# One more attention stack beside layer 1's dispatch, and one attention step of layer 0 ahead of its first expert block

## The chip, the cores and the metric

The kernel runs on one core of one Trainium2 chip. The metric is the device time of one execution in microseconds. The core has five engines that each work through their own queue of instructions in order: TensorE (PE, with its weight loads as PEld), VectorE (DVE), ScalarE (ACT), GpSimd (POOL) and SyncE (SP, which here only issues transfers). Engines wait for one another by semaphores. Transfers (DMA) are issued by SP, ACT or POOL and then run on their own.

## The reference, cut to what matters

The input x has 32 sequences of 256 tokens with 128 features, so 8192 tokens. Two layers follow one another, each of the form x + s·silu(g), where s is an attention and g a mixture of experts, both on the normalised x:

```
xn = layernorm(x)
s  = L0 attention(xn)          # 16 heads of 8; product of two causal score matrices, no softmax
g  = silu(L0 experts(xn))      # 8 experts, the top 2 per token, plus a shared expert
x  = x + s * g
xn = layernorm(x)
s  = L1 attention(xn)          # 16 heads of 8; every 4th key and the keys within 8, softmax
g  = silu(L1 experts(xn))      # 8 experts, the top 2, at most 2048 tokens each
x  = x + s * g
```

In both layers the attention needs nothing of that layer's routing, and the experts need nothing of its attention. Only the last line of a layer joins them.

## The kernel before, in words

Tokens are handled in 16 packs of 512 (two sequences each). All of a layer's expert work goes through memory: each token's normalised row is scattered to the slots of its two experts (`disp0` in layer 0, `disp` in layer 1), the expert blocks read these slots, and their results are scattered back (`moe0`, `moe`) and read again by the step that combines them.

**Layer 0.** `attention0` (line 850) is a generator cut into 256 steps, eight for each sequence. `step()` (line 1032) runs one of them and counts it in `at`. The program strews these steps over the other work: two for each pack after the first while packs are loaded and normalised (30 steps), 12 beside the routing, then 103 beside the dispatch (line 1079, 128 indirect scatters issued by POOL, a step behind four of every five), then 71 beside the experts (line 1085, a step at every fourth yield of `experts()`), and the last 40 with `combine0` of the packs. The step run at yield 0 of the experts is number 145 counted from 0. Within sequence 18 it is the second of eight steps: it finishes sequence 17 (the 16 value matmuls of line 813, the copy `yT` of line 838, the output projection of line 842, the copy of line 844 and, as 17 is the second sequence of its pack, the 512 KB write of `part`, issued by ACT, line 847) and it starts the projections of sequence 19 (matmuls of line 727 and the two DVE products of line 732).

`experts()` (line 914) works off 71 blocks of 256 rows. Block i first transposes its rows (`xdt`, line 926), copies them (`xdT`, line 928) and yields. Then come the up matmuls (`eup`, line 935) with their activations (`ha`, line 940), and the down matmuls of the block before (`edn`, line 948). `fetch` (line 902) brings a block's weights by an indirect transfer from POOL and its rows by SP. The rows wait for all 128 scatters (`out0.behind(get)`, line 911). The transposes of block 0 are set behind the last ordered matmul that PE got so far (line 924).

**How the order is set.** Most instructions pass through `inline` (line 256), which ties each to the one before it on its engine, so that these stay in the order in which the program gives them. The rest is placed by a planner. In layer 1 the order of PE is exactly that of the program (`manual_schedule`).

**Layer 1.** `Attention` (line 287) works in 64 *stacks* of 128 query rows, two for each sequence, each advanced by `next(att.steps)` and counted in `begun`. Stack n computes the scores of its own rows (`apsc`, lines 378 and 384), their softmax weights (DVE lines 395 and 396, ACT line 398), and finishes stack n−1: transposes `apsT` (line 406), copies `apT` (line 408), value products `apav` (line 415). Along the way it prepares the next sequence (`prepare`, line 317). In the first stack of a sequence this includes the four DVE products `akb` (line 347), behind the stack's softmax work. Eight stacks run beside the end of layer 0, four beside `route1`, and 34 beside the dispatch (loop of line 1162, three or four scatters issued for each), so that `begun` is 46. The scatters go out three at a time, and POOL waits for the three before (`pace`, line 146).

Then come the 32 expert blocks of layer 1 (line 1169), with no attention beside them. Each block reads its rows by SP once all scatters have landed (line 1176), and its PSUM tiles (pool `pm`) take the banks that the scores had (pool `ps_s`, closed at line 1166). Last come the 18 stacks that are left, beside `combine` (line 1225) of the 16 packs. `combine` has three parts: reading the result rows, then sum and tanh, then products and output. The sums and products are on POOL (on DVE for the last pack), the tanh on ACT. Its buffers are three deep. `plan` (line 1250) says behind which of the remaining stacks each part stands: pack p of the first 12 at int(p·gap)+0, +2 and +3 with gap = (64 − begun)/13, the others at (4p − begun)+2, +6 and +7 (for pack 12 this is 4, 8 and 9). ACT and DVE take the parts in that order, between the stacks' own instructions.

Of the kernel before, what the change touches and what calls it, by code (L numbers as in the profile page):

```python
# [51 lines left out]
def some(g, n):  # L52
    for _ in range(n):
        next(g, None)
# [3 lines left out]
def model_kernel(ctx: ExitStack, tc: tile.TileContext, a: dict, out: bass.AP):  # L58
# [483 lines left out]
    with ExitStack() as c0:  # L542
# [155 lines left out]
        def dispatch():  # L698
            for k in range(2):
                if k:  # L700
                    nc.gpsimd.tensor_scalar(xr[:, :, P], xr[:, :, P], float(-T), None, ALU.add)
                    nc.gpsimd.tensor_copy(xr[:, :, P + 1], gate0[:, 1, :])
                for n in range(NT):
                    out0.put(slot0[:, k, n : n + 1], xr[:, n, :], NB * TB)
                    yield
# [111 lines left out]
        def shared(p, so):  # L817

            hs = ka.tile([P, NFC, PT], F32, tag="hs", name="hs", bufs=1)
            for f in range(NFC):  # L820
                psu = mm_tile("psu")
                inline(nc.tensor.matmul(psu, lhsT=upw[:, f * P : (f + 1) * P], rhs=xTs[p],
                                 start=True, stop=True))
                inline(nc.scalar.activation(hs[:, f, :], psu, AF.Gelu, bias=upb[:, f : f + 1]))
                yield
            dn = mm_tile("dn").rearrange("p (i c) -> p i c", i=TT)
            for i in range(TT):
                for f in range(NFC):
                    inline(nc.tensor.matmul(dn[:, i, :], lhsT=hs[:, f, i * P : (i + 1) * P],
                                     rhs=dnw[:, f, :], start=(f == 0), stop=(f == NFC - 1)))  # L830
            inline(nc.vector.scalar_tensor_tensor(so[:, 1], dn, 0.1, bc(dnb, 1, TT), ALU.mult, ALU.add))
            yield
# [199 lines left out]
        def step():  # L1032
            nonlocal at, sh
            p, n = at // 16, at % 16
            if n == 0:
                sos[p] = kso.tile([P, 2, TT, P], F32, tag="so", name="so")
                sh = shared(p, sos[p])
            next(gen)
            if n % 2 == 0:
                some(sh, 1)  # L1040
            if n == 15:
                for _ in sh:
                    pass
            at += 1
# [4 lines left out]
        BLOCK = 4  # L1049
# [29 lines left out]
        for n, _ in enumerate(dispatch()):  # L1079
            if n % 5 != 4:  # L1080
                step()
            if n % 8 == 0:
                some(wipe, 1)
        ek = ce.enter_context(tc.tile_pool(name="ek0", bufs=2))
        for n, _ in enumerate(experts()):
            if n % BLOCK == 0:
                step()
        ce.close()
        bk = c0.enter_context(tc.tile_pool(name="bk0", bufs=4))
# [7 lines left out]
        begun = 0  # L1097
# [19 lines left out]
        att = Attention(ctx, {p: sres[:, p * TT : (p + 1) * TT, :] for p in range(EARLY)})  # L1117
# [19 lines left out]
    def dispatch1(m):  # L1137
        for k, n in todo[:m]:
            if (k, n) == (0, 0):
                nc.gpsimd.tensor_scalar(xr[:, :, P], xr[:, :, P], float(T), None, ALU.add)  # L1140
                nc.gpsimd.tensor_copy(xr[:, :, P + 1], gate[:, 0, :])
            out1.put(sidx[:, k, n : n + 1], xr[:, n, :], E * CAP)
        del todo[:m]
# [17 lines left out]
    with tc.manual_schedule(engines={mybir.EngineType.PE}):  # L1161
        while todo:
            dispatch1(4 if len(todo) > NT // 4 else 3)
            next(att.steps)
            begun += 1
    cs1.close()


# [191 lines left out]
```

## Time and profile before

| what | us |
|---|---|
| median of 4 runs | 1935.88 (1916.36, 1935.78, 1935.98, 1937.61) |
| the profiled execution, its own time | 1940.79 |
| its span, first to last instruction | 1939.0 |
| PE busy | 1805.0 (93% of the span) |
| DVE busy | 1177.1 (61%) |
| ACT busy | 961.9 (50%) |
| POOL busy | 849.2 (44%) |
| layer 0's experts begin on PE | 459.88 |
| layer 1's experts begin on PE | 1525.16 |
| the last 18 stacks begin on PE | 1769.82 |

A line of the timeline has the start and the length of an instruction in us, its engine, its line in the kernel, the operation, what it writes and reads, its shape, a count where like ones were merged, and in brackets how long the engine sat idle before and who released it. A line of the table by stretches has the stretch, its length, then busy time and number of instructions of PE, PEld, DVE, ACT and POOL, the clock that PE was granted (1.00 is full speed), the busy share of the DMA engines, and GB/s. The last scatter is followed by the issue of the first row reads on SP (SPq).

### The profile page before, as it was taken

What the parts mean: (1) busy time and instruction counts of PE and PEld (TensorE: products, weight loads), DVE (VectorE), ACT (ScalarE), POOL (GpSimd) and SP (SyncE); (2) the same over time, 40 slices, a digit from 0 to 9 for tenths busy, and PEclk for the clock granted to TensorE, in tenths of its full rate; (3) what the DMA queues carried; (4) which work ended last, traced back from release to release, by engine and by line L of the source; (5) the groups of instructions that cost most, each with busy time, mean ns of one, the idle gap of its engine ahead of it and who ended that gap; (6) DMA issues with size and microseconds to landing.
All of it is one profiled execution on the core that took longest, in us unless ns stands there. A gap on an engine that the chain in (4) does not pass through costs nothing.

```text
span 1939.0 us, 45909 instructions
## 1 busy us (share of the span) xinstructions
PE 1805.0 (93%) x18616; PEld 1394.5 (72%) x18616; DVE 1177.1 (61%) x2227; ACT 961.9 (50%) x2180; POOL 849.2 (44%) x991
## 2 busy tenths in 40 slices
PE   5999999997999999999887799999999799999997
PEld 4777777775888878888765576677777576777665
DVE  6659667664333334433577587888888433335886
ACT  5433333333444444545354475567767333335776
POOL 3001554553444454544545530044554355554554
PEclk8999999998999999999988877899999899999988
DMA  8911111112343443434334410121011122222333
GB/s 282 382 49 37 62 56 41 43 44 63 119 149 123 127 142 119 150 123 137 117 104 142 139 48 7 62 74 35 31 34 33 54 70 68 72 67 84 100 113 90
DMA packets 127524, 183.86 MB, mean 95 GB/s; under 512 B 16340, under 2 KB 83183, under 8 KB 127312
## 3 DMA queue, kind: packets, MB, share of 16 engines
q1 hardware_dynamic: 96096, 92.45, 16.2%
q0 software_dynamic: 28336, 79.73, 12.3%
q10 hardware_dynamic: 2880, 8.74, 1.2%
q8 instruction: 147, 2.41, 0.5%
q14 instruction: 65, 0.53, 0.1%
HBM read 104.11 MB, written 78.00 MB: 94 GB/s over the span
## 4 chain that ended last, share of the span: by engine, by line
PE 31%; ACT 7%; DVE 6%; DMA 2%; issue 2%; POOL 2%; SPq 0%; ACTq 0%; DVEq 0%; POOLq 0%
PE mpsu L1186 6%; PE mpsd L1200 6%; PE apsc L378 3%; PE apsT L406 3%; ACT apT L408 3%; PE apav L415 3%; ACT apr L398 2%; PE apsc L384 1%; PE apsk L338 1%; DMA rows<-moe 1%; PE apsq L350 1%; PE apsv L358 1%; DVE apr L396 1%; PE mpst L1179 1%; DVE amx L395 1%
## 5 line engine op out<-in xcount | busy, mean ns | idle before, releaser
L166 POOL DMA_INDIRECT moe<-od,to x270 | 269.8, 999 | 124.8 <-issue 71.1
L777 ACT COPY qk<-ptr 128x512 f32<-128x512 f32 x256 | 138.1, 588 | 242.0 <-PE ptr L775 241.7
L792 DVE TENSOR_TENSOR pat<-pp,dmask 128x1024 f32<-128x1024 f32 x128 | 156.4, 1222 | 109.9 <-PE pp L790 109.9
L408 ACT COPY apT<-apsT 124x512 f32<-124x512 f32 x256 | 143.1, 584 | 102.9 <-PE apsT L406 102.0
L395 DVE TENSOR_REDUCE amx<-apsc 128x4 f32<-128x496 f32 x256 | 170.6, 666 | 38.0 <-PE apsc L384 37.9
L790 PE MATMUL pp<-qk 64*128 64x128 f32 x2048 | 172.6, 297 | 17.0 <-DVE pat L792 15.3
L790 PEld LDWEIGHTS pp<-qk 64*128 64x128 f32 x2048 | 136.9, 194 | 59.6 <-issue 43.1
L396 DVE TENSOR_TENSOR apr<-apsc,amx 128x496 f32<-128x496 f32 x256 | 172.6, 674 | 9.0
L940 ACT ACTIVATE ha<-eup,wt 128x256 f32<-128x256 f32 x284 | 119.0, 471 | 111.9 <-PE eup L935 58.2
L166 POOL DMA_INDIRECT disp<-xr,slot x128 | 134.1, 1048 | 62.8 <-POOL breath L150 26.1
L744 DVE TENSOR_TENSOR feat<-rot 128x1024 f32<-128x1024 f32 x128 | 158.6, 1280 | 3.9
L935 PE MATMUL eup<-xdT,wt 128*128 128x256 f32 x568 | 150.3, 390 | 10.9 <-ACT od L954 6.8
L406 PE MATMUL apsT<-ident,apr 128*124 128x128 f32 x1024 | 150.5, 293 | 9.6 <-ACT apr L398 4.9
L775 PE MATMUL ptr<-ident,feat 128*128 128x128 f32 x1024 | 146.9, 287 | 8.0 <-DVE feat L744 8.0
L166 POOL DMA_INDIRECT disp<-xr,sidx x128 | 126.7, 990 | 55.1 <-POOL breath L150 25.5
L415 PE MATMUL apav<-ava,apT 124*64 124x9 f32 x4096 | 142.6, 205 | 0.0
L415 PEld LDWEIGHTS apav<-ava,apT 124*64 124x64 f32 x4096 | 136.0, 139 | 8.8 <-issue 8.6
L948 PEld LDWEIGHTS edn<-wt,ha 128*128 128x128 f32 x1136 | 137.8, 192 | 3.6
L948 PE MATMUL edn<-wt,ha 128*128 128x128 f32 x1136 | 138.1, 275 | 0.0
L775 PEld LDWEIGHTS ptr<-ident,feat 128*128 128x128 f32 x1024 | 114.8, 145 | 30.2 <-issue 13.7
L406 PEld LDWEIGHTS apsT<-ident,apr 128*124 128x124 f32 x1024 | 121.3, 148 | 17.5 <-ACT apr L398 10.2
L935 PEld LDWEIGHTS eup<-xdT,wt 128*128 128x128 f32 x568 | 99.7, 190 | 45.0 <-issue 27.7
(250 smaller groups left out, 3344.7 us busy)
## 6 DMA issues: line engine op xcount, KB each, us to landing
disp<-zero SPq DMA_DIRECT2D x17, 1040.0 KB, 8.3
rows<-moe SPq DMA_DIRECT2D x64, 256.0 KB, 5.2
xd<-disp SPq DMA_DIRECT2D x71, 130.0 KB, 2.3
xd<-disp SPq DMA_DIRECT2D x32, 260.0 KB, 2.8
x<-in_x SPq DMA_DIRECT2D x32, 256.0 KB, 4.5
moe<-zero SPq DMA_DIRECT2D x8, 1024.0 KB, 14.9
part<-so ACTq DMA_DIRECT2D x16, 512.0 KB, 3.4
soin<-part SPq DMA_DIRECT2D x16, 512.0 KB, 4.4
```

Of the source, the lines that this page charges most:

```text
L166: ins = order(lambda: nc.gpsimd.indirect_dma_start(out=self.dst[:, :], out_offset=bass.IndirectOffsetOnAxis(ap=idx, axis=0), in_=rows, in_ ...
L395: inline(nc.vector.tensor_reduce(mx, sv, AX.X, ALU.max))
L396: inline(nc.vector.tensor_tensor(to, sv, bc(mx, 2, NK), ALU.subtract))
L406: nc.tensor.transpose(psT[:NK, j, :], pr[:, 4 * g + j, :], ident)
L408: inline(nc.scalar.copy(pT[:NK], psT[:NK]))
L415: nc.tensor.matmul(avv[u * QB : (u + 1) * QB, h, :], lhsT=pT[:NK, j, u * QB : (u + 1) * QB], rhs=va[:NK, 2 * st + u, h, :], start=True, st ...
L744: inline(eng.tensor_tensor(f[:, n].rearrange("p (h i j) -> p h i j", i=D, j=D), bc(r[:, n], 3, D), bc(r[:, 2 + n], 2, D), ALU.mult))
L775: inline(nc.tensor.transpose(pst[:, 2 * n + c], seq.feat[c][:, n, m * P : (m + 1) * P], ident))
L790: inline(nc.tensor.matmul(pp[:, w, i, c], lhsT=qk[r, 2 + c], rhs=qk[r, c], start=True, stop=True))
L792: inline(nc.vector.tensor_tensor(pat.rearrange("p w i c q -> p (w i c) q"), pp.rearrange("p w i c q -> p (w i c) q"), bc(dmask, 1, 8), ALU ...
L935: nc.tensor.matmul(pu, lhsT=wt[:, f * P : (f + 1) * P], rhs=xdT, start=True, stop=True)
L948: nc.tensor.matmul(psd[:, s, :], lhsT=hl[:, f, s * P : (s + 1) * P], rhs=wl[:, FF + f * P : FF + (f + 1) * P], start=(f == 0), stop=(f == ...
```

## The change

One step of layer 0's attention, number 145, is put in front of the experts (and in front of the pool that they open) and taken away at their yield 0. All later steps stay where they were. In layer 1 one stack, number 46 counted from 0, is put behind the dispatch loop, in front of the expert blocks. It is the first stack of a sequence. The remaining 17 stacks then run at the end, with `begun` at 47, from which `plan` is worked out anew.

```
                 step()
             if n % 8 == 0:
                 some(wipe, 1)
+        step()
         ek = ce.enter_context(tc.tile_pool(name="ek0", bufs=2))
         for n, _ in enumerate(experts()):
-            if n % BLOCK == 0:
+            if n and n % BLOCK == 0:
                 step()
...
             dispatch1(4 if len(todo) > NT // 4 else 3)
             next(att.steps)
             begun += 1
+
+        next(att.steps)
+        begun += 1
     cs1.close()
```

More of the change, by code (lines that the diff above doesn't have):

```diff
@@ L1083, in model_kernel @@
                 some(wipe, 1)
+        step()
         ek = ce.enter_context(tc.tile_pool(name="ek0", bufs=2))
         for n, _ in enumerate(experts()):
-            if n % BLOCK == 0:
+            if n and n % BLOCK == 0:
                 step()
@@ L1165, in model_kernel @@
             begun += 1
+        next(att.steps)
+        begun += 1
     cs1.close()
```

## The prediction

> **What bounds the kernel now.** I read the page first: PE is busy 1805.0 of 1939.0 us, so time is won where PE idles or where work comes off its path. The table of busy time by stretches shows where it idles.
>
> ```profile
> 450.00:460.00 10.00, 0.12 (x1) 0.16 (x2) 0.00 (x0) 0.52 (x1) 3.54 (x6) 0.70 0.22 59
> 460.00:945.00 485.00, 474.13 (x4017) 396.16 (x4018) 184.42 (x299) 233.64 (x585) 226.84 (x280) 1.00 0.40 126
> ...
> 1514.00:1525.00 11.00, 0.04 (x1) 0.00 (x0) 1.36 (x4) 1.08 (x3) 3.93 (x5) 0.57 0.21 66
> 1525.00:1770.00 245.00, 244.84 (x1410) 175.49 (x1411) 88.82 (x127) 80.16 (x188) 125.92 (x154) 0.99 0.23 66
> 1770.00:1939.00 169.00, 147.91 (x2086) 109.18 (x2084) 130.47 (x248) 119.97 (x245) 83.78 (x67) 0.92 0.36 104
> ```
>
> There are two holes of 10 and 11 us, each just ahead of a stage of experts. These stages are PE-bound (474 of 485 us, 245 of 245), so a later or earlier start is carried through them. The last stretch is not full: PE 148 of 169 us. The timeline shows what ends the first hole.
>
> ```profile
> 452.99 0.10 POOL L150 MEMSET breath<- 128x1 f32 x1 [1.36 <-DMA disp<-xr,slot]
> ...
> 454.99 0.97 POOL L166 DMA_INDIRECT disp<-xr,slot  x1 [0.30 <-issue]
> 457.62 37.65 SPq L910 DMA_DIRECT2D xd<-disp  x8
> ...
> 459.88 0.66 PE L926 MATMUL xdt<-ident,xd 128*128 128x128 f32 x2 [10.08 <-DMA xd<-disp]
> ...
> 460.46 1.08 PE L813 MATMUL y<-pat,vz 128*32 128x128 f32 x16
> ...
> 464.20 1.94 PE L935 MATMUL eup<-xdT,wt 128*128 128x256 f32 x8
> ```
>
> PE waits for the last scatter and the rows behind it. Then step 145 (from 460.46) stands between the transposes and the first up matmuls. The second hole:
>
> ```profile
> 1512.05 1.98 PE L415 MATMUL apav<-ava,apT 124*64 124x9 f32 x60
> ...
> 1519.76 0.98 POOL L166 DMA_INDIRECT disp<-xr,sidx  x1 [0.63 <-POOL breath L150]
> 1522.41 26.86 SPq L1175 DMA_DIRECT2D xd<-disp  x6
> ...
> 1525.16 1.94 PE L1179 MATMUL mpst<-ident,xd 128*128 128x128 f32 x8 [11.12 <-issue]
> ```
>
> The stacks end at 1514.03 and the rows come at 1525.16. The scatters are paced by their own landings (three per 5.7 us or more), not by the stacks.
>
> **The step.** It removes nothing; step 145 moves from behind the first transposes into the hole. On PE it is 16 value, 2 projection and 4 output matmuls. A like step at full clock (431.84 on) shows 0.64, 1.13 and 0.61 us, about 2.4; at 460.46, after the hole, they take 1.08, 2.08 and 1.06. Without it the up matmuls could start when xdT is copied (460.57 + 0.42, and 0.2 for the signal: 461.2) instead of about 464.0: 2.8 us. PE was slow there, until about 465.7, and the hole that is left (some 7 us) is long enough for the same to follow. The slow time then falls on other work, and only the step's full-clock price counts: 2.8 × 2.38/4.22 = 1.6 us. So the gain lies between 1.6 and 2.8; I take 2.0.
>
> On DVE its two products (1.29 us) come off 463.59 into idle time (DVE had idled 11.4 us); on ACT two copies of 0.37 us likewise. No POOL or SP instruction moves: expert weights were asked for from 188.2 on, and the row reads on SP wait for the scatters alone. But the step issues one transfer, the 512 KB write of part on ACT's queue, so far at 464.85, now at about 452.6, beside the last two scatters (issued 453.72 and 454.99). Six such writes stand within the dispatch (204.36, 245.68, 286.99, 328.30, 369.70, 411.00). POOL's next wait for its scatters was 1.50, 2.98, 3.58, 3.27, 1.69 and 1.66 us, where about 1.5 is the rule: 0 to 2.1 more, 0.95 on average. The row reads come later by that much; I take 1.0. Net −1.0 us, bounds −2.8 and +0.5 (−1.6 + 2.1).
>
> **The stack.** Stack 46 leaves the end, where it runs from 1769.82 to 1777.63 (7.8 us), and enters the second hole. Its like is the stack at 1498.12, also the first of a sequence: PE runs 8.2 us, the last softmax product on DVE ends 8.6 after the start, akb 10.1, the last DVE product (ao) 10.6. From 1514.1 this gives PE free at 1522.3, the score banks (which the expert tiles take over) free at 1522.7, DVE free at 1524.7. The rows arrive at 1525.16 and DVE is first wanted at 1526.28. The cover is the wait for the last scatter; the margins are 2.8, 2.4 and 1.6 us. Without the cover, were the rows there at 1514, the move would cost what it saves. It adds no transfer and no POOL work, and its akb starts (1522.6) after the last scatter was issued. So the experts start as before, and 7.8 us go at the end.
>
> Does PE start faster, with 2.8 us of hole instead of 11? After the 11 us the first 8 transposes took 1.94 us (later 4 take 0.60) and the first three up matmuls 2.38 (later 1.29): 0.74 + 1.09 = 1.8 us to win, 2.0 with the signal waits. The nearest row is the 1.78 us pause of PE at 1843.7: 16 score matmuls after it still took 1.48 instead of 1.09 us. I take 0, bounds −2.0 and 0.
>
> [...]
>
> **The combines.** What is late next is the end. gap falls from 18/13 to 17/13, and 16 combines lie over 17 stacks. Worked out from plan, the tanh parts of packs 0 to 11 stood behind stacks 2, 3, 4, 6, 7, 8, 10, 11, 13, 14, 15, 17 and those of 12 to 14 behind 8, 12, 16: one pair, at 8. Now they stand behind 2, 3, 4, 5, 7, 8, 9, 11, 12, 13, 15, 16 and 7, 11, 15: three pairs. The pair at 8 is visible:
>
> ```profile
> 1842.41 1.09 PE L406 MATMUL apsT<-ident,apr 128*124 128x128 f32 x8
> 1843.34 0.39 PE L426 MATMUL apsf<-wqkvo,aoT 128*128 128x128 f32 x2
> 1845.51 0.70 PE L350 MATMUL apsq<-axT,wqkvo 128*128 128x256 f32 x2 [1.78 <-ACT apT L408]
> ...
> 1849.54 1.97 PE L406 MATMUL apsT<-ident,apr 128*124 128x128 f32 x8 [1.00 <-DVE s L427]
> ```
>
> ```profile
> 1826.27 1.63 DVE L347 TENSOR_SCALAR akb<-akT,hmask 128x496 f32<-128x496 f32 x4
> ...
> 1843.46 4.67 DVE L347 TENSOR_SCALAR akb<-akT,hmask 128x496 f32<-128x496 f32 x4
> ```
>
> ACT does two tanh parts in a row and PE waits 1.78 us for apT. The same akb that takes 1.63 us takes 4.67 while POOL runs its sums and products. That stack lasts 13.1 us (1842.41 to 1855.52), where one of its kind lasts 7.7: 5.4 lost. A tanh part alone costs some 0.5 (8.7 against 8.2). The akb also meets POOL at 1899.37, without a pair. In the changed kernel pairs 7 and 11 stand behind a stack with akb, pair 15 does not (its stack is of the last sequence). Of the two added pairs each costs at least 1.78 − 2 × 0.5 = 0.8 and at most 5.4. I take 1.0 each, nearer the low end, since the akb met POOL at 1843.46 through a sum that had waited for a buffer (1843.54), not through the pair's own products, which began at 1845. So +2.0; bounds +10.8, and −8.4 if stack 55's 5.4 and the 3.0 on the other slow akb go away.
>
> **Sum**, on the profiled execution (1940.79; its span is 1939.0, 1.8 lies around it): −1.0 + 0 − 7.8 + 2.0 = −6.8, so 1934.0. The median of the four runs shown is 4.9 lower than the profiled one; against it I forecast 1935.9 − 6.8 = 1929.1, or 1929.
>
> **Rivals.**
> - *The end gives it back.* The combines, not PE, set the end: POOL waits 18.7 us there for buffers and 16.7 for rows. For it: PE is busy 148 of 169 us. Against: 15 of the 18 stacks last 7.3 to 9.0 us, near their undisturbed 7.7 to 8.2. With pairs costing 5 to 8 in all it ends between 1932 and 1936.
> - *Slower.* Both added pairs cost what stack 55 lost, 10.8 us. It decides from 8.8 on (7.8 + 1.0). Price: −8.8 + 10.8 = +2.0, so 1938. For it: the only pair on show cost just that. Against: see the akb above.
> - *Lucky phases.* The slow akbs vanish (−8.4 instead of +2.0) and PE starts warm (−2.0): down to 1917, or 1923 with half of it. For it: akb met POOL at only 2 of 8 places.
> - *The step does nothing.* The part write eats it all; +1.0 on my forecast, inside its range.
>
> **How the numbers follow.** Chances: forecast 0.5 (own range 1924 to 1933), given back 0.2, slower 0.15, lucky 0.15. The bounds add up to −2.8 − 2.0 − 7.8 − 8.4 = −21.0, so 1915, and +0.5 − 7.8 + 10.8 = +3.5, so 1939.4. I cut a little below and take 1917 to 1940. About 1% (19 us) is what a measurement of this kernel can tell from no change, as one of the four runs lies 1% under the others. Over 1% faster needs under 1916.5: the far end of the lucky case and that scatter of runs, 0.11. Over 1% slower (1955) is beyond all bounds, 0.04 for what I overlooked. The rest, 0.85, is within 1%.
>
> **What would show it.** Step: y, psp and pso of step 145 right behind 450, the first eup about 1.3 us after the transposes instead of 4.3, the row reads on SP 0 to 2 us later after the last scatter's issue. Stack: the hole ahead of mpst under 4 us, the experts' 245 us unchanged, 17 stacks behind them. Clock: the first 8 mpst in 1.9 us or 1.1. End: the stacks behind slots 7 and 11 over 9 us, akb at 1.63 or 4.7. The forecast is wrong if rows wait for the stack's DVE work, or if the end stretch shortens by less than 4 us.

## The result and the profile after

The changed kernel takes 1926.35 us (median of 44 runs, 1914.65 to 1938.23), the kernel before 1929.41 in 70 runs beside it: ratio 0.9987, interval 0.9976 to 0.9999, so −2.5 us (−4.6 to −0.2) where −6.8 was forecast. The forecast time of 1929 lies nearer than that, and this is luck: it started from the median of four runs, 1935.88, which is 6.5 above that of the 70. Single executions of one kernel scatter by about 5 us (standard deviation of the 44). The two profiled ones, 1939.0 and 1929.7 us of span, differ by 9.3, so no single stage of one trace proves a difference of a few us.

The stretches of the changed kernel that answer to those shown of before (length, then busy time of PE, PEld, DVE, ACT, POOL, PE's granted clock, DMA share, GB/s):

```profile
451.50:462.00 10.50, 0.03 (x1) 0.07 (x2) 0.83 (x2) 0.35 (x1) 3.10 (x5) 0.75 0.31 101
462.00:942.50 480.50, 469.80 (x3966) 392.70 (x3966) 181.53 (x295) 230.94 (x578) 223.83 (x278) 0.99 0.40 126
1513.50:1522.00 8.50, 7.82 (x109) 5.47 (x109) 6.86 (x15) 6.11 (x13) 2.05 (x3) 0.99 0.24 72
1522.00:1768.00 246.00, 245.59 (x1407) 175.49 (x1408) 90.51 (x134) 80.16 (x188) 125.87 (x154) 0.99 0.23 65
1768.00:1929.70 161.70, 140.71 (x1980) 104.84 (x1979) 122.80 (x232) 114.58 (x234) 83.72 (x67) 0.92 0.38 109
```

The second hole is full (PE 7.82 of 8.50 us), the experts behind it take the same 246 us, and the end is shorter by 7.6 (161.6 from the first of its stacks at 1768.14 to the end of the span, 169.2 before). The first hole is as long as before. Its timeline:

```profile
451.73 0.97 POOL L166 DMA_INDIRECT disp<-xr,slot  x1 [0.31 <-issue]
451.88 0.33 ACTq L847 DMA_DIRECT2D part<-so  x1
454.96 0.10 POOL L150 MEMSET breath<- 128x1 f32 x1 [2.27 <-DMA disp<-xr,slot]
...
456.97 0.97 POOL L166 DMA_INDIRECT disp<-xr,slot  x1 [0.30 <-issue]
459.79 1.77 SPq L910 DMA_DIRECT2D xd<-disp  x4
...
461.97 0.66 PE L926 MATMUL xdt<-ident,xd 128*128 128x128 f32 x2 [10.52 <-DMA xd<-disp]
...
462.55 1.65 PE L790 MATMUL pp<-qk 64*128 64x128 f32 x12
464.14 1.22 PE L935 MATMUL eup<-xdT,wt 128*128 128x256 f32 x2
```

The write of part goes out beside the last scatters, and POOL's wait for them is 2.27 us (1.36 before). The step is gone from behind the transposes, but the planner now puts twelve score products (`pp`) of step 146 there. The first up matmul follows 2.2 us after the transposes: not 4.3 as before, nor 1.3 as forecast. The second hole:

```profile
1519.55 1.75 SPq L1179 DMA_DIRECT2D xd<-disp  x4
...
1519.71 2.04 PE L415 MATMUL apav<-ava,apT 124*64 124x9 f32 x64
...
1521.36 0.68 DVE L396 TENSOR_TENSOR apr<-apsc,amx 128x496 f32<-128x496 f32 x1
...
1522.32 0.19 POOL L184 TENSOR_SCALAR to<-xd 128x4 int32<-128x4 f32 x1 [4.43 <-DMA xd<-disp]
1522.33 1.94 PE L1183 MATMUL mpst<-ident,xd 128*128 128x128 f32 x8 [0.58 <-DVE apr L396]
```

The expert transposes wait 0.58 us. The trace names the stack's last softmax product, but that had ended 0.3 us before. POOL's first work on the rows (`to`, line 184), which waits for them alone, starts at 1522.32, and the transposes 0.01 behind it, as in the trace of before (1525.15 and 1525.16). So here too the rows came last, by a little.

### The profile page after: what moved, and what is told of

It reads as the page before. It is cut to its first block, busy times and chain, and to the rows that moved or that the text cites. A ratio compares the mean times of both kernels' runs of the same rounds, so it can differ in the third digit from the quotient of the medians.

```text
span 1929.7 us, 45913 instructions
## 1 busy us (share of the span) xinstructions
PE 1809.3 (94%) x18616; PEld 1396.1 (72%) x18616; DVE 1175.0 (61%) x2227; ACT 961.9 (50%) x2180; POOL 850.6 (44%) x991
## 4 chain that ended last, share of the span: by engine, by line
PE 31%; ACT 8%; DVE 6%; DMA 2%; issue 2%; POOL 2%; SPq 0%; ACTq 0%; DVEq 0%; POOLq 0%
PE mpsu L1190 6%; PE mpsd L1204 6%; PE apsc L378 4%; PE apsT L406 3%; PE apav L415 3%; ACT apT L408 3%; ACT apr L398 2%; PE apsc L384 2%; PE apsk L338 2%; PE apsq L350 1%; DMA rows<-moe 1%; PE apsv L358 1%; DMA soin<-part 1%; DVE apr L396 1%; DVE amx L395 1%
```

## The experiments

Each set of four ran on one chip, with the kernel before beside it.

**First set: the parts alone.** Stack alone, step alone (the two hunks of the diff), and two variants:

```
  # e3_nopairs, on the changed kernel: due times of packs 12 to 15
-... for p in range(EARLY - 1, NP) for t in (2, 6, 7)]
+... for p in range(EARLY - 1, NP) for t in (2, 5, 7)]
  # e4_step_write_later, on the step alone
-            if b % 2:
+            if b == 17:
+                held.append(p)
+            elif b % 2:
...
+            if n == 1:
+                nc.scalar.dma_start(part[held[0]], sos[held[0]])
```

> The stack alone is moved, the step stays behind the first transposes. As forecast (the move is covered by the wait for the last scatter, the end loses a stack and pays 2 us for pairs): 5.8 us under the kernel before. Rival, the cover is too short: the row reads come before the stack's last softmax product has freed the banks in this execution, the first transposes wait for DVE, and only 2 to 4 us are gained. In the trace the two are told apart by what the first transposes of layer 1's experts waited for.

> The step alone is moved. As forecast: 1.0 us under the kernel before, the row reads on SP 1 us later after the last scatter than before. Rival, the step gives nothing: the write of part delays the rows by 2 us and the first six score matmuls of the next step stand ahead of the first up matmuls, so that the first down matmuls come at the same time or up to 1 us later than before: 0 to 1 us over it.

> The changed kernel, but the tanh parts of packs 12 to 15 stand one stack earlier (slots 6, 10 and 14, which no other pack has). If the pairs cost 1 us each and what they bring on the products akb: 2 to 3 us under the changed kernel, 5 us under the kernel before, no stack over 9.5 us at the end. If pairs cost nothing beyond single parts: as the changed kernel, within 1 us.

> The step alone is moved, and the 512 KB write that it issues is held back until the first block of the experts has its transposes. If that write delays the last scatters: the row reads on SP come 1 to 2 us earlier after the last scatter's issue than with the step moved and the write in it, and the time is 1 to 2 us under that. If the write is harmless there: both as with the step moved.

Measured, against 1928.43: stack 0.9956 (0.9933 to 0.9979), −8.5 us; step 0.9977 (0.9956 to 0.9999), −4.4; no pairs 0.9943 (0.9921 to 0.9966), −11.0; write later 0.9995 (0.9974 to 1.0015), −1.0. Each part gains alone, the step by little: its interval barely leaves 1, and the fourth, which moves the step too, stands at −1.0. The fourth says nothing on the write: its trace has it at 452.4, half a us later than in the changed kernel, where the row reads had already gone out at 451.99.

The no-pairs trace shows the first hole when the dispatch ends early: SP issues the row reads at 451.45.

```profile
450.83 0.61 PE L842 MATMUL pso<-wout,yT 128*128 128x128 f32 x4
453.74 0.41 PE L926 MATMUL xdt<-ident,xd 128*128 128x128 f32 x2 [2.31 <-DMA xd<-disp]
454.08 0.94 PE L790 MATMUL pp<-qk 64*128 64x128 f32 x12
454.95 1.35 PE L935 MATMUL eup<-xdT,wt 128*128 128x256 f32 x5
```

The hole left is 2.3 us, PE keeps full clock (12 `pp` in 0.94 us, not 1.65), and the up matmuls follow after 1.2 us. The row reads of layer 0 stood at 448.9 to 459.8 in ten traces (before, the changed kernel and the first two sets), whether the step was moved or not; they go 1.7 to 2.3 us after the last scatter's issue ended. From the first transposes to the last down matmul of layer 0 it is 480.5 to 483.0 us with the step behind (four traces, mean 482.1) and 477.8 to 480.9 with it in front (six, mean 479.5).

**Second set: pairs and cover.** The changed kernel again, the stack alone without pairs (2, 5, 7), the kernel before with that same edit, which makes three pairs there out of one, and the changed kernel with one stack more:

```
  # e7_two_stacks, on the changed kernel
-        next(att.steps)
-        begun += 1
+        for _ in range(2):
+            next(att.steps)
+            begun += 1
```

> The changed kernel once more, beside e5 to e7 and the kernel before on one chip. If its parts add up as measured singly (stack alone 0.9956, step alone 0.9977), it stands at 0.993, some 13 us under before. Rival: the two parts spoil each other (a later start of dispatch 1 or another phase of the end), and it stays at the 0.9987 of its first measurement. Its end stretch should again last 159 to 162 us, with three stacks behind slots 7, 11 and 15 over 9 us.

> The stack alone, with the tanh parts of packs 12 to 14 one slot earlier (6, 10, 14), so that no slot has two. If pairs cost 1.0 each, as the prediction took them, it is 3 us under the stack alone (1921.2, so 1918). Rival, by the granted clock: each pair makes a pause of 1 to 1.5 us, after which the clock is at a half for a stretch of 3.41 us, and PE loses half of it besides the pause: 2.5 to 3 us for a pair, so 7 us under the stack alone, 1914. The end stretch would last 159 or 155 us, and at most two stretches at half clock would lie in it, where the stack alone has four.

> The kernel before with this one edit to the due times, which there makes three pairs (slots 7, 11, 15) out of one (slot 8): two pairs added, and nothing else. If a pair costs 1.0: 2 us over before. By the clock rival: 5 to 6 us over before. By the prediction's slower rival (5.4 each): 10.8 over. If pairs cost nothing and e3_nopairs was fast for another reason, the same as before.

> The changed kernel with a second stack behind the dispatch's last: the cover is used up by the first (PE had 0.6 us left). The second stands bare in the hole, the experts start some 8 us later than in the changed kernel and the end is one stack shorter, so it takes the same time within 2 us. Rival, cover left: if the row reads arrive later than the stacks' end, up to 3 us of the second is hidden too and it is faster by as much. Rival, a third: the combines, now one for each of 16 stacks, hold the end back, and it is slower by 3 us or more.

Measured, on this chip against 1926.82: changed 0.9974 (0.9956 to 0.9992), −5.0 us; stack without pairs 0.9948 (0.9924 to 0.9972), −10.0; pairs alone 0.9997 (0.9976 to 1.0018), −0.6; two stacks 0.9982 (0.9960 to 1.0003), −3.5. So the parts do not add up to 0.993 in the changed kernel. The edit of the due times by itself gains nothing in the kernel before, although it takes three tanh parts one slot forward. And the second stack stands bare: from the start of the second dispatch to the expert transposes it is 273.7 to 276.1 us with one stack (five traces), 271.8 to 276.1 without (four), and 283.2 with two, 8.7 more than the mean of one (274.5, and 274.15 without). In its trace the rows are ready long before:

```profile
1510.55 3.32 SPq L1180 DMA_DIRECT2D xd<-disp  x4
...
1523.11 1.98 PE L415 MATMUL apav<-ava,apT 124*64 124x9 f32 x60
1526.05 1.61 PE L1184 MATMUL mpst<-ident,xd 128*128 128x128 f32 x8 [0.96 <-DVE apr L396]
```

What it costs there it saves at the end, as expected.

**Third set: the same on another chip, and six pairs.** The changed kernel, the stack alone, no pairs, and this:

```
  # e8_six_pairs, on the changed kernel
-... (int(p * gap) + t, p) for p in range(EARLY - 1) for t in (0, 2, 3)]
+... (int(p * gap) + t + (t > 0 and p % 2 == 0), p) for p in range(EARLY - 1) for t in (0, 2, 3)]
```

> The changed kernel, on one chip with the stack alone, the changed kernel without pairs and one with six pairs. So far it stood at 0.9987 and 0.9974 of before, while its stack alone stood at 0.9956 and itself without pairs at 0.9943. If the parts add up, it stands 1 to 3 us under the stack alone here. Rival, the parts spoil each other: 3 us or more over the stack alone.

> The stack alone once more, on the same chip as the changed kernel. 0.9956 before; by the stage times (one stack of 7.8 us less at the end, two added pairs at about 1 to 2.5 each) 0.997 to 0.9985. If it stands at 0.9956 again and the changed kernel at 0.998, the moved step costs time where the stack is moved too.

> The changed kernel without pairs once more, on the same chip as the changed kernel. If a pair costs 1.0, it is 3 us under it; if each costs a pause and half of a stretch of 3.41 us at half clock, 6 to 8 us under it. If pairs cost nothing, as e6_pairs_alone (0.9997) would have it, the same.

> The changed kernel with the tanh and product parts of every other one of packs 0 to 11 one slot later, which makes six pairs (3, 5, 8, 11, 13, 16) out of three. At 1.0 a pair 3 us over the changed kernel; by the clock rival 6 to 8 us over it; the same, if pairs cost nothing. The stacks behind those slots should show the two tanh parts in a row and a pause of PE of 1 us or more.

On this chip the kernel before took 2016.05 us, 4.6% more than on the others. Against it: changed 1.0038 (1.0018 to 1.0058), +7.7 us; stack alone 1.0046 (1.0026 to 1.0065), +9.3; no pairs 0.9997 (0.9976 to 1.0019), −0.6; six pairs 1.0035 (1.0015 to 1.0055), +7.1. So the change is slower here; stack and changed kernel are alike; the due times without pairs are worth 8.3 us; three pairs more cost nothing. All four traces, which are of changed kernels, show why the moved work gains nothing: in each the rows are there 85 to 91 us before the experts start. The changed kernel on this chip, beside the second dispatch, up to the rows and from there to the experts:

```profile
1253.50:1515.00 261.50, 222.37 (x2631) 160.32 (x2632) 161.33 (x320) 130.11 (x262) 131.94 (x174) 0.82 0.16 52
1515.00:1608.00 93.00, 89.04 (x1225) 66.67 (x1225) 74.44 (x150) 62.08 (x128) 0.87 (x4) 0.93 0.04 13
```

and the same stage of the changed kernel in its first trace:

```profile
1248.50:1512.00 263.50, 252.31 (x3713) 188.66 (x3713) 225.67 (x454) 183.34 (x374) 129.36 (x170) 0.99 0.15 51
```

The scatters take as long, but PE does 2631 matmuls in that time in place of 3713. It is idle for 39 us (11 in the other), and its clock is 0.82: half clock for some 94 of the 261 us, which by the halved pace is worth 47 (an estimate). Its value products stop in mid-stack, released by nothing that the trace names:

```profile
1306.10 1.52 PE L415 MATMUL apav<-ava,apT 124*64 124x9 f32 x45
1308.02 0.32 PE L415 MATMUL apav<-ava,apT 124*64 124x9 f32 x5 [0.40 <-issue]
1308.77 0.33 PE L415 MATMUL apav<-ava,apT 124*64 124x9 f32 x4 [0.44 <-issue]
```

For the matmuls of line 415 such waits add up to 23.4 us between 1250 and 1512 here (23.2 to 24.8 in the four), and to nothing in the first trace. 23 stacks (1472 value products by 64) are done when the rows come, where the other has 33, and the experts begin 93 us after the reads go out. There is no hole to put a stack into. The first hole is gone as well: the reads go out at 454.06, PE ends the moved step at 468.2 and the transposes are held up by it. Here the two moves together are worth nothing (0.9997), and what the slots of the tanh parts cost is left to be paid. What makes PE wait for issue on this chip stays open.

## Why the prediction was right or wrong

**The step: −1.0 taken.** Right as far as the runs can tell. The stage of layer 0's experts is 2.5 us shorter by the means above (2.0 taken). The first up matmul came 1.2 us after the transposes, near the sign of 1.3, only where the hole was short and the clock full (e2, e3, e4; in e3 2.31 us and 1.00); where it was long and the clock at a half it came after 2.2 (both traces of the changed kernel, e7; in the changed kernel's first 10.52 us, and 0.50 until 467.05). In the trace of before the half clock ended at 464.30, a little ahead of the 465.7 that the prediction read from durations. The stage's start is later by 1.3 in the mean (456.0 to 457.3, leaving out e4), where 1.0 was taken for the write; single starts range over 11 us, so this difference isn't shown. Alone the step gives −4.4 (−8.5 to −0.2), which holds −1.0.

**The stack hidden: 0 taken.** Right in two of the five traces with one stack and a hole to put it in: the changed kernel's first and e1. In the other three, e3, r2 (the changed kernel's repeat) and e5, the transposes start 2.7, 2.4 and 2.7 us after POOL's first work on the rows, and 0.06 after the stack's last softmax product, so the start waits for the stack's DVE work, which was one of the prediction's signs of being wrong. In r2:

```profile
1510.75 0.19 POOL L184 TENSOR_SCALAR to<-xd 128x4 int32<-128x4 f32 x1 [5.30 <-DMA xd<-disp]
...
1512.37 0.67 DVE L396 TENSOR_TENSOR apr<-apsc,amx 128x496 f32<-128x496 f32 x1
...
1513.10 1.09 PE L1183 MATMUL mpst<-ident,xd 128*128 128x128 f32 x8 [0.34 <-DVE apr L396]
```

The margins of 1.6 to 2.8 us were worked out from one execution, and that one had the longest hole: without the stack it lasts 11.12 us in the trace of before, but 9.30, 8.19 and 5.62 in e2, e4 and e6, and the stack needs 8.6 up to its last softmax product. The first hole ranges as widely, from 1.65 to 10.08 us with the step behind it. So 0 was too low for the stack by 1.5 us in the mean of the five traces, though the scatter of the dispatch hides this: in the mean of the stages above the start moved by +0.4 us (274.15 to 274.54). On the third chip the cover is gone, and the move costs what it saves, as the prediction put it for rows that are there at 1514. That PE's pace beside the dispatch could be that of another chip was in no rival.

**The clock: 0 taken.** Right in this trace, for the wrong reason. The pause is down to 0.58 us, and the first 8 transposes still take 1.94 us. The clock fell to a half at the end of the stack (1521.77), not after a pause; in the 3.41 us ahead PE was busy for 3.38:

```profile
1518.36:1521.77 3.41, 3.38 (x68) 2.52 (x68) 3.31 (x6) 2.42 (x6) 0.00 (x0) 1.00 0.40 112
1522.00:1523.00 1.00, 0.67 (x4) 0.70 (x4) 1.00 (x4) 0.00 (x0) 0.19 (x1) 0.50 1.03 268
```

In the trace of the stack without pairs it did not fall:

```profile
1515.45 1.09 PE L1182 MATMUL mpst<-ident,xd 128*128 128x128 f32 x8 [0.34 <-DVE apr L396]
1517.71 7.13 PE L1189 MATMUL mpsu<-xdT,w 128*128 128x512 f32 x16 [1.17 <-DVE xdT L1184]
```

There the 16 up matmuls take 7.13 us (9.23 in the changed kernel) and the expert stage 243.97 (245.81). This is the 1.8 us that the prediction named, but the pause alone doesn't decide it: in e1 and e3, with pauses of 0.67 and 0.35 us, the first 3 us of the experts ran at half clock, and behind waits of 0.34 and 0.35 us on the third chip the first 8 transposes took 1.09 us in two traces (stack alone, six pairs) and 1.91 and 1.96 in the other two.

**The end: −7.8 taken.** Right. In the same ten traces, with 16, 17 or 18 stacks left, the length from the first to the last matmul of the end follows 6.2 + 8.0 × stacks + 0.98 × (1 − granted clock) × length, within 1.7 us in nine of them (−4.6 in e5; a fit by least squares, with the clock to two digits). For instance the changed kernel and the kernel without pairs:

```profile
1768.14:1921.55 153.41, 140.57 (x1979) 104.70 (x1977) 119.74 (x227) 113.32 (x232) 83.58 (x67) 0.94 0.39 112
```
```profile
1757.60:1906.10 148.50, 136.91 (x1979) 102.42 (x1977) 120.06 (x227) 113.47 (x232) 82.93 (x67) 0.97 0.42 117
```

A stack less is worth 8.0. The second term is half clock, by this fit worth half of the time that it lasts. It lasts 8.9 to 21.6 us of the end in these ten traces, so it costs 4.4 to 10.8 us, as the execution has it.

**The pairs: +2.0 taken.** This is the term that was mis-sized, as what the new due times cost. The slots 7, 11, 15 against 6, 10, 14 cost 8.3 us on the third chip; elsewhere the changed kernel stands 8.5 (first measurement) and 6.0 (second) above the one without pairs, by their ratios to the kernel before in different sets; the two forms of the stack alone differ by 1.5, on two chips. The step that failed is the reading of stack 55's 5.4 us as a pair (pause) plus an akb that met POOL. Three things were in it. First, the pause of two tanh parts (1.52 us, at 1838.09) is that of two single ones (0.76 each) and no more. The waits of PE in the changed kernel:

```profile
1810.33 0.44 PE L327 MATMUL apst<-ident,xr 128*128 128x128 f32 x2 [0.76 <-ACT apT L408]
1822.88 0.33 PE L421 MATMUL apso<-ident,ao 128*128 128x128 f32 x1 [1.52 <-DVE sres L427]
1838.09 0.70 PE L350 MATMUL apsq<-axT,wqkvo 128*128 128x256 f32 x2 [1.52 <-ACT apT L408]
1846.58 0.44 PE L327 MATMUL apst<-ident,xr 128*128 128x128 f32 x2 [0.76 <-ACT apT L408]
```

Second, the slow akb is real (4.68 us at 1817.45, and 1.52 of wait behind it at 1822.88), but the kernel without pairs has as many slow ones (4.67, 4.21, 2.85) and is faster. Third, the clock stood at a half from 1846.7 to 1853.5 in the trace of before, 6.8 us in which PE lost up to 3.4: that is what "lasts 13.1" held beside the pause. With pairs, half clock lasts 18.4, 21.6 and 18.1 us of the end, without 8.9 and 17.6; on the third chip 32.3 and 36.1 against 25.2 (worked out from the clock to two digits). By half of that, the slots cost 3.1 and 4.5 us in the mean, and PE's idle time adds 2.6 (11.9 against 9.3) and 0.8 (15.9 against 15.1): 5.7 and 5.3 from these single traces. But half clock doesn't follow the number of pairs: it lasts 19.3 us in the kernel before with one, 9.3 in e6 with three, and 22.5 in e8 with six.

**What stays open.** That two tanh parts in one slot are the cause is not shown: pairs added cost nothing (e6: −0.6 with two more, e8: −0.6 against the changed kernel with three more), although in e8 the pauses of 1.52 us are there, four times. The edit of the due times also moves three tanh parts from behind the first stack of a sequence (54, 58, 62) to behind the second of the one before (53, 57, 61), in e3, e5 and e6 alike; the runs don't part that from the pairs, and it may be what counts. And the stack alone on the first chip (−8.5, with three pairs) is faster than the changed kernel ever was (−2.5, −5.0); their intervals meet, and on the third chip the two are equal.

**The rivals.** *The end gives it back* comes nearest: it put pairs at 5 to 8 us in all, and −1.0 − 7.8 + 6 would be −2.8. But that the combines set the end isn't shown: what follows the last matmul is 8.0 to 8.2 us in nine of the ten traces, with and without pairs. *Slower* came true on one chip, by a lost cover as well as by the tanh slots. The lowest of the versions on both chips where it ran is the one without pairs: 0.9943 on the first, 0.9997 on the third.

## What to carry to other kernels

Work that is moved into a hole is worth the hole that each execution and each chip has, so read the hole from several executions, and ask what sets both ends of it (here scatters at one, PE's pace at the other) and what happens if either moves by a tenth. Where a trace names who ended a wait, see that this one ended just before. Before a slow stretch is put down to an instruction pattern, read the granted clock over just that stretch: a repeat may not have it (the first 8 transposes of layer 1's experts took 1.94 us in one trace of the changed kernel, 1.09 in another). When a planner spreads side work over what is left, changing what is left moves all of it, and that can be worth as much as the move itself.

## What the runs showed of the hardware

**Half clock also came behind stretches in which PE was busy nearly throughout.** Two such places in the changed kernel's end:

```profile
1849.45:1852.86 3.41, 3.28 (x63) 2.42 (x64) 3.34 (x6) 2.42 (x7) 3.33 (x3) 1.00 0.01 2
1852.86:1856.27 3.41, 3.41 (x24) 2.93 (x21) 3.34 (x8) 2.79 (x6) 2.20 (x3) 0.50 0.76 222
1856.27:1859.68 3.41, 3.28 (x38) 2.11 (x39) 2.22 (x5) 1.91 (x5) 3.33 (x4) 1.00 0.27 85
...
1866.51:1869.93 3.42, 3.24 (x60) 2.28 (x58) 3.35 (x6) 2.43 (x6) 0.12 (x1) 1.00 0.02 5
1869.93:1873.34 3.41, 3.27 (x29) 2.94 (x26) 3.01 (x9) 3.41 (x8) 1.13 (x1) 0.50 0.00 0
1873.34:1876.75 3.41, 3.41 (x21) 1.09 (x22) 0.14 (x2) 1.25 (x3) 3.41 (x4) 0.50 0.57 170
```

PE was busy 3.28 and 3.24 us in the rows directly ahead of both, so hardly a pause lay in these; in the stretch of 1852.86 it was busy throughout (3.41 us), and its eight transposes at 1853.29 take 1.97 us (1.16 at 1844.43, at full clock). The first stretch of half clock lasted 3.41 us, the second 6.82 (to 1876.75), and in this trace they began 17.07 us apart, five times 3.41 within rounding. The two others of this end, from 1825.55 and from 1917.71, came behind 2.67 of 3.42 and 2.55 of 3.41 us of busy PE. What made the clock fall is not shown.

**The same program runs at another pace on another chip**: 2016 against 1927 and 1928 us for the kernel before. In the four traces taken there, all of changed kernels, PE waits 23.2 to 24.8 us for issue at the value products beside the second dispatch, and not at all there in the first trace.
